# First-layer experts: unscaled tokens against four experts at once, gates applied to the products by VectorE, the eight products summed by GpSimd

## The chip, the cores and the metric

The kernel runs on one core of a Trainium2 chip. The core has a matrix engine (TensorE, "PE" in the profile; its weight loads are "PEld"), a vector engine (VectorE, "DVE"), a scalar engine (ScalarE, "ACT"), GpSimd ("POOL") and SyncE ("SP"), which here only issues DMAs. Every engine works through its own queue in order. The metric is device microseconds of one execution, and the time of a kernel is the median of its runs.

## The reference, cut to what matters

The input is `x`, 32 images of 56 x 56 pixels with 128 channels in float32, which is 100,352 tokens. Two layers follow each other; each is a mixing step and a feed-forward step with residual sums. The change is in the feed-forward step of the first layer, a mixture of eight experts of which each token uses two:

```python
router_probs = softmax(x @ router_w + router_b)          # x: tokens after a layer norm
top_p, top_i = top_k(router_probs, 2)
top_p = top_p / sum(top_p)
expert_out = einsum('bnd,edc->bnec', x, expert_w) + expert_b   # 8 experts, 128 -> 128
gathered   = take_along_axis(expert_out, top_i[..., None], axis=2)
out        = einsum('bnk,bnkc->bnc', top_p, gathered)
t = t + out
```

The kernel computes all eight experts for every token and lets the gates of the six unused ones be zero, so that for a token n the result is the sum over e of gate[n, e] * (x[n] @ expert_w[e]). Around this step lie, in the first layer, a 3 x 3 convolution of signs after a batch norm over the whole input, and in the second layer a triangle product per image and a second set of experts that pick tokens.

## The kernel before, in words

The tokens are cut into 112 units of 896 tokens, and a unit into seven tiles of 128 tokens (`N7 = 7`). Seven units are a pair of images. A first pass over all units computes the statistics of the batch norm; it ends at about 350 us. Then come 16 pairs, which overlap like a pipeline, and at the end the experts of the second layer for all images.

The order of the instructions on each engine is not that of the code. Every stage registers operations with `@op(engine, cost in ns, reads, writes)`, and a planner (class `Order`) simulates the engines with these costs, takes the ready operation of the smallest rank, and writes out the fixed order. The ranks come from the table `TICK`, one number per stage and unit, with 14 ticks from one pair to the next. Buffers come from tagged pools: eight PSUM banks (`ps`), five tiles of 128 x 1024 float32 (`gb`), five unit tiles (`u`), twelve `x` tiles, and so on; an operation whose tile finds no free buffer waits.

For a pair the stages that matter here are:

- `moe_stats` (statistics by `bn_stats`, L484, and a chain of small VectorE instructions, L504 to L546), `moe_turn` (ScalarE normalizes, L558, TensorE transposes, L473, ScalarE copies to `xT`, L579), and `moe_route`, which ends with `gg`, the gates of 14 x 128 tokens for eight experts, tokens on the partitions.
- `moe_gates`, once a unit: TensorE transposes the unit's gates (L793), ScalarE copies them (L800) and issues a DMA to `gate_d` in device memory.
- `moe_experts`, once a tile, so 784 times: a DMA brings the tile's gates back into a `gb` buffer, repeated on all 128 partitions (512 KB each). VectorE multiplies this in place by the transposed tokens (L823). Then eight matmuls, one per expert, add up in PSUM (L828); the scaled tokens are the stationary side and the expert's 128 x 128 weights the moving side. Four tiles share one PSUM bank.
- `moe_add`, twice a unit: VectorE adds the PSUM bank to the residual `x` (L840).

The second layer follows with `tri_stats` and `gate_stats` (the same statistics chains as `moe_stats`), `sign` (VectorE writes the signs into a frame, L607, for the convolution at L629), `tri_out` (L1098, L1107), and `top8`. GpSimd has, in each pair, one memset of `zv` (L1035), one of `a_bd` (L1114) and eight row gathers (L1229), and after the pairs the scatter DMAs of the last experts (L1497). The second layer's experts (`late_experts`) keep their weights in `gb` and `x` buffers and scale rows by `gains` (L1480).

The preparation of the weights makes `expert_w` as one 128 x 1024 tensor, the eight experts side by side; its averages use matmuls with 512 moving columns (L1800).

Of the kernel before, what the change touches and what calls it, by code (L numbers as in the profile page):

```python
# [27 lines left out]
C = 128  # L28
# [9 lines left out]
TICK = {  # L38
    "fetch": (1.14, 2.61, 2.37, -0.16, 7.91, 9.69, 13.32),
    "sign": (0.38, 0.8, 0.81, 5.7, 6.62, 8.09, 11.62),  # L40
    "conv": (2.4, 3.69, 6.8, 7.72, 10.43, 11.89, 12.86),
    "conv_back": (2.88, 4.08, 7.34, 7.86, 10.43, 11.92, 14.91),
    "moe_turn": (4.53, 5.17, 9.52, 8.55, 12.68, 12.47, 15.14),
    "moe_gates": (6.43, 7.52, 9.89, 10.15, 13.98, 12.85, 16.56),
    "moe_experts": (7.18, 7.67, 10.31, 10.83, 14.93, 12.94, 16.8),
    "moe_add0": (10.78, 13.85, 13.48, 12.98, 18.39, 17.9, 18.29),
    "moe_add1": (10.06, 12.78, 13.45, 11.14, 15.45, 13.84, 17.8),
    "tri_turn": (15.73, 17.37, 18.31, 18.26, 19.34, 19.61, 19.71),
    "moe_stats": (4.26, 8.17, 12.25, 14.94),
    "moe_route": (5.48, 9.71, 12.84, 15.88),  # L50
    "tri_stats": (14.82, 13.52, 18.41, 19.02),
    "tri_b": (19.79, 19.99),
    "tri_a": (19.82, 21.57),
    "tri_z": (21.72,),
    "tri_out": (22.38, 23.42, 24.57, 25.03, 26.33, 28.33, 30.18),
    "gate_stats": (23.97, 24.69, 27.63, 30.31),
    "gate_turn": (25.8, 26.15, 26.94, 28.19, 29.43, 32.04, 32.1),
    "gate_logits": (25.91, 27.01, 28.84, 29.87, 31.66, 33.33, 32.83, 33.54),
    "clear": (31.73,),
    "top8": (34.46,),  # L60
    "pool_rows": (37.33,),
    "late_first": (37.82, 37.92, 38.25, 41.79, 42.31, 42.85),
    "late_alone": (51.08, 41.11, 38.24, 41.73, 42.93, 41.08),
    "late_rest": (39.41, 40.01, 40.1, 40.59, 42.76, 44.26, 47.21, 48.79, 50.74, 58.57),
    "last_sums": (49.02,),
    "last_rows": (63.85,),
}
# [216 lines left out]
def kernel(ctx: ExitStack, tc: tile.TileContext, a: dict, out: bass.AP):  # L284
# [101 lines left out]
    z_d = [dram.tile([NV, CH, N7, 2 * H], F32, name=f"z_{p}") for p in range(NP)]  # L386
    gate_d = [dram.tile([N7, E0, 128], F32, name=f"gate_{g}") for g in range(NUT)]

# [14 lines left out]
    with ExitStack() as c2:  # L403
# [19 lines left out]
        for t in lines:  # L423
# [4 lines left out]
            "st": 3, "q": 3, "rT": 1, "lg": 2, "k1": 2, "k2": 2, "mk": 2, "d": 2,  # L428
            "gg": 2, "gT": 2, "rm": 4, "abm": 2, "b": 1, "zq": 1, "zT": 1, "lgT": 1,
            "m8": 2, "i8": 2, "sq": 2, "pg": 2, "near": 2, "pacc": 1, "ptc": 1, "pt": 1,  # L430
# [253 lines left out]
        def moe_route(p, m):  # L684
# [81 lines left out]

            @op("ACT", 210, r=[d], w=[(d, 1)])
            def _():
                nc.scalar.activation(d.ap[:, 1, :], d.ap[:, 0, :], AF.Sigmoid)
                nc.scalar.activation(d.ap[:, 2, :], d.ap[:, 0, :], AF.Sigmoid, scale=-1.0)  # L770
# [11 lines left out]

        def moe_gates(p, u):

            name = f"{p}_{u}"
            m, j = batch_of(u)
            gg = live[p]["gg", m]
            trg = bank(f"trg_{name}")
            gT = new("gT", [N7 * E0, 128], f"gT_{name}")

            @op("PE", 110, r=[gg], w=[trg])
            def _():
                nc.tensor.transpose(  # L793
                    trg.ap[: N7 * E0, :128],
                    gg.ap[:, j * N7 : (j + 1) * N7, :].rearrange("p n e -> p (n e)"), ident,
                )

            @op("ACT", 150, r=[trg], w=[gT])
            def _():
                nc.scalar.copy(gT.ap, trg.ap[: N7 * E0, :128])  # L800

            @op("ACT", 330, r=[gT], w=[("gd", p, u)], land=300)
            def _():
                nc.scalar.dma_start(gate_d[p * NU + u].rearrange("n e q -> (n e) q"), gT.ap)

        def moe_experts(p, u, n):

            name = f"{p}_{u}_{n}"
            xT = live[p]["xT", u]
            if n % 4 == 0:  # L810
                live[p]["acc", u, n // 4] = bank(f"acc_{name}")
            acc = live[p]["acc", u, n // 4]
            gb = new("gb", [C, E0, 128], f"gb_{name}")

            @op("SP", 360, r=[("gd", p, u)], w=[gb], land=1300)
            def _():
                nc.sync.dma_start(
                    gb.ap, gate_d[p * NU + u][n].unsqueeze(0).to_broadcast([C, E0, 128])
                )

            @op("DVE", 1130, r=[(xT, n)], w=[gb])
            def _():
                nc.vector.tensor_tensor(gb.ap, gb.ap, over(xT.ap[:, n, :], E0), ALU.mult)  # L823

            @op("PE", 227 * E0, r=[gb], w=[(acc, n % 4)])
            def _():
                for e in range(E0):
                    nc.tensor.matmul(  # L828
                        acc.ap[:, n % 4 * C : (n % 4 + 1) * C], lhsT=gb.ap[:, e, :],
                        rhs=expert_w[:, e * C : (e + 1) * C], start=(e == 0), stop=(e == E0 - 1),  # L830
                    )

        def moe_add(p, u, q):
            x_, acc = live[p]["x", u], live[p].pop(("acc", u, q))
            k = (4, 3)[q]

            @op("DVE", 60 + 134 * k, r=parts(acc, k), w=parts(x_)[4 * q : 4 * q + k])
            def _():
                dst = x_.ap[:, 4 * q : 4 * q + k, :].rearrange("p n c -> p (n c)")
                nc.vector.tensor_tensor(dst, acc.ap[:, : k * C], dst, ALU.add)  # L840

# [81 lines left out]
        def tri_b(p, h):  # L923

            if h == 0:
                live[p]["b"] = new("b", [128, CH, W], f"b_s_{p}")
            b_s = live[p]["b"]
            u = gated_half(p, "b", h, wb, bb)

            @op("ACT", 540, r=[(u, 0), (u, 4)], w=[(b_s, h)])  # L930
            def _():
                ns = slice(4 * h, min(4 * h + 4, N7))
                nc.scalar.activation(
                    b_s.ap.rearrange("p c (v n) -> p c v n", n=N7)[:, :, :, ns],
                    u.ap[:, :, : (4, 3)[h], :].rearrange("p v n c -> p c v n"), AF.Sigmoid,
                )

        def tri_a(p, h):

            u = gated_half(p, "a", h, wa, ba)  # L940

            @op("ACT", 2 * 500, r=[(u, 0), (u, 4)], w=[("a_bd", h)])
            def _():
# [8 lines left out]
        def tri_z(p):  # L952
# [94 lines left out]
            for j in range(2):  # L1047
                @op("ACT", 750, r=[(zv, rg) for rg in range(4)],
                    w=[("zc", j), ("a_bd", j)])
                def _(j=j):  # L1050
                    nc.scalar.copy(zc[:, j], zv.ap[:, :, j, :].rearrange("c v h -> c h v"))
# [123 lines left out]
        def top8(p):  # L1175
# [32 lines left out]

            @op("ACT", 2700, r=[q, m8], w=all_lg + [(q, 1), (pg, 1)])
            def _():  # L1210
# [725 lines left out]
        for p in range(NP):  # L1936
            for u in range(NU):
# [4 lines left out]
                put(p, "moe_turn", u, moe_turn, p, u)  # L1942
                put(p, "moe_gates", u, moe_gates, p, u)
                for n in range(N7):
# [78 lines left out]
```

## Time and profile before

| what | value |
|---|---|
| median of three runs | 3841.74 us (3836.13 to 3844.88) |
| the profiled execution | 3851.35 us, span 3849.5 us |
| instructions in the span | 77,967 |
| first pass, to about 351 us | PE busy 311.02 us, DVE 299.92 us of 351 us |
| pairs, 351 to 3448 us | PE busy 2940.51 us, DVE 2733.22 us, ACT 1937.06 us, POOL 156.02 us of 3097 us |
| end, from 3448 us | PE busy 244.17 us, DVE 115.92 us, POOL 238.55 us of 401.5 us |
| mean granted TensorE clock | 0.958 of full speed |
| DMA | 811.90 MB in the span; the 784 gate loads are 512 KB each |

Busy time of an engine is the time in which at least one of its instructions was under way; instructions overlap a little at their ends, so that the distance from start to start is below an instruction's own duration. "Idle before" is the time in which the engine had nothing under way, with the event that ended it. The stretch of a pair can be read from the memset at L1114, which comes once a pair: its starts at 838.85 us and 3384.50 us lie 13 pairs apart, 195.8 us each.

### The profile page before, as it was taken

Reading aid. Unit: us, or ns where it says so; the run is one execution under the profiler, and the core shown is the slowest. Engines: PE = TensorE matmul, PEld = TensorE weight load, DVE = VectorE, ACT = ScalarE, POOL = GpSimd, SP = SyncE. Lnnn points to the kernel's source line nnn. Section 1 sums busy time; section 2 is a strip of 40 time slices with the busy share of each in tenths; the row PEclk is TensorE's granted clock in tenths of the full one; section 3 lists DMA queues with packets and bytes.
Section 4 is the critical chain, followed back from the end, with each engine's and each line's share of the span. In section 5 each row is a group of like instructions: output and inputs, shape, how many; then the busy total and the mean of one; then the engine's idle time right before and its main releaser. Section 6 shows DMA issues by size and latency. Waiting matters only on the chain.

```text
span 3849.5 us, 77967 instructions
## 1 busy us (share of the span) xinstructions
PE 3495.7 (91%) x27661; PEld 2836.7 (74%) x27661; DVE 3149.1 (82%) x10452; ACT 2355.4 (61%) x5458; POOL 407.0 (11%) x472
## 2 busy tenths in 40 slices
PE   7999999999999999999999999999999999997653
PEld 6886787777777777778787868686878787865442
DVE  7997879898989898989898989898989898875310
ACT  5997437566666666675757575757575747566210
POOL 1000000100000000000000000101010101003667
PEclk9999999999999999999999999999999999998776
DMA  7997556465656565656565656565656565656774
GB/s 252 349 342 257 199 176 243 174 235 183 230 183 229 176 225 186 224 190 220 191 224 188 219 182 223 188 230 189 230 189 218 201 217 203 203 195 187 211 199 73
DMA packets 325544, 811.90 MB, mean 211 GB/s; under 512 B 86170, under 2 KB 110659, under 8 KB 325155
## 3 DMA queue, kind: packets, MB, share of 16 engines
q1 hardware_dynamic: 262034, 680.39, 51.4%
q10 hardware_dynamic: 41104, 109.20, 7.3%
q0 software_dynamic: 22016, 17.32, 3.1%
q8 instruction: 220, 3.60, 0.4%
q14 instruction: 170, 1.38, 0.1%
HBM read 630.19 MB, written 176.55 MB: 210 GB/s over the span
## 4 chain that ended last, share of the span: by engine, by line
PE 39%; DVE 33%; ACT 11%; DMA 9%; issue 4%; POOL 3%; ACTq 0%; another core or an unknown queue 0%; SPq 0%; DVEq 0%; POOLq 0%
PE acc L828 22%; DVE stln L484 8%; DVE gb L823 7%; DMA gb<-gate 4%; DVE sg L1098 3%; PE ps_cv L629 3%; DMA out<-eo_False,picked 3%; PE gram L1673 3%; POOL out L1497 2%; PE tr L473 2%; DVE x L1107 2%; DVE x L571 2%; ACT ym L558 1%; ACT yt L558 1%; PE ps_z L972 1%
## 5 line engine op out<-in xcount | busy, mean ns | idle before, releaser
L828 PE MATMUL acc<-expert_w,gb 128*128 128x128 f32 x12544 | 1443.9, 276 | 25.2 <-DVE gb L823 13.5
L828 PEld LDWEIGHTS acc<-expert_w,gb 128*128 128x128 f32 x12544 | 1415.1, 192 | 67.3 <-DVE gb L823 33.9
L823 DVE TENSOR_TENSOR gb<-gb,xT 128x1024 f32<-128x1024 f32 x784 | 949.4, 1217 | 64.5 <-DMA gb<-gate 61.5
L484 DVE BATCH_NORM_STATS2 stln<-x 128x6 f32<-128x128 f32 x2352 | 576.4, 281 | 1.9
L558 ACT ACTIVATE ym<-x,rmln 128x128 f32<-128x128 f32 x784 | 322.4, 486 | 244.4 <-DVE rmln L546 243.6
L629 PE MATMUL ps_cv<-frame,w_sign 128*128 128x448 bf16 x2016 | 427.5, 362 | 8.4 <-DVE frame L607 8.4
L558 ACT ACTIVATE yt<-x,rmln 128x128 f32<-128x128 f32 x784 | 324.5, 486 | 123.2 <-DVE rmln L546 120.0
L558 ACT ACTIVATE yl<-x,rmln 128x128 f32<-128x128 f32 x784 | 318.6, 487 | 125.9 <-DVE rmln L543 113.3
L629 PEld LDWEIGHTS <-w_sign 128*128 128x128 bf16 x2016 | 196.4, 99 | 188.5 <-issue 23.8
L1229 POOL DMA_INDIRECT rows<-y,near x128 | 122.2, 955 | 1113.5 <-DVE mk L730 1007.0
L1114 POOL MEMSET a_bd<- 128x2048 f32 x16 | 29.5, 1841 | 1846.3 <-PE ps_zo L1085 1400.7
L840 DVE TENSOR_TENSOR x<-acc,x 128x512 f32<-128x512 f32 x224 | 137.9, 616 | 95.7 <-PE acc L828 95.6
L1497 POOL DMA_INDIRECT out<-eo_False,picked x128 | 197.1, 1540 | 139.0 <-DMA out<-eo_False,picked 74.8
L558 ACT ACTIVATE y<-x,rm 128x128 f32<-128x128 f32 x448 | 194.7, 486 | 20.2 <-DVE rm L543 11.3
L637 ACT ACTIVATE cv<-ps_cv,cv_shift,cv_scale 128x448 f32<-128x448 f32 x224 | 157.9, 725 | 74.8 <-PE ps_cv L629 74.3
L1063 PEld LDWEIGHTS ps_g<-wg,yT 128*128 128x128 f32 x1568 | 187.7, 193 | 21.6 <-issue 15.1
L1063 PE MATMUL ps_g<-wg,yT 128*128 128x128 f32 x1568 | 203.5, 280 | 0.0
L484 DVE BATCH_NORM_STATS2 st<-x 128x6 f32<-128x128 f32 x784 | 179.6, 278 | 24.5 <-DMA x<-in_x 24.2
L1673 PE MATMUL gram<-y 128*128 128x128 f32 x1568 | 196.7, 278 | 0.0
L1673 PEld LDWEIGHTS gram<-y 128*128 128x128 f32 x1568 | 192.3, 198 | 0.0
L579 ACT COPY xT<-trm 128x512 f32<-128x512 f32 x224 | 108.6, 528 | 98.9 <-PE trm L473 79.4
L473 PE MATMUL tr<-ident,y 128*128 128x128 f32 x784 | 139.2, 295 | 29.1 <-ACT y L558 23.1
(244 smaller groups left out, 5295.0 us busy)
## 6 DMA issues: line engine op xcount, KB each, us to landing
gb<-gate SPq DMA_DIRECT2D x784, 512.0 KB
x<-in_x SPq DMA_DIRECT2D x224, 448.0 KB
y<-yT SPq DMA_DIRECT2D x112, 448.0 KB
ys<-y SPq DMA_DIRECT2D x112, 448.0 KB
out<-x ACTq DMA_DIRECT2D x112, 448.0 KB
y<-yl ACTq DMA_DIRECT2D x112, 448.0 KB
w_False<-in_L_ffn_weight SPq DMA_DIRECT2D x128, 256.0 KB
w_True<-in_L_ffn_weight SPq DMA_DIRECT2D x48, 256.0 KB
```

Source lines behind the costliest of these rows:

```text
L473: nc.tensor.transpose(ps.ap[:, n * 128 : (n + 1) * 128], get()[:, n0 + n, :], ident)
L484: nc.vector.bn_stats(st.ap[:, c0 + k, :], src.ap[:, k, :])
L558: nc.scalar.activation(dst.ap[:, k, :], src.ap[:, k, :], AF.Identity, bias=m, scale=r)
L629: nc.tensor.matmul(acc, lhsT=w_sign[:, tap, :], rhs=frames[f][:, 8 * band + kh : 8 * band + kh + 8, kw : kw + W], start=(tap == 0), stop=( ...
L637: nc.scalar.activation(cv.ap[:, :, 64 * h : 64 * h + 64], ps.ap[:, :448].rearrange("c (q n) -> c n q", n=N7), AF.Identity, bias=cv_shift, ...
L823: nc.vector.tensor_tensor(gb.ap, gb.ap, over(xT.ap[:, n, :], E0), ALU.mult)
L828: nc.tensor.matmul(acc.ap[:, n % 4 * C : (n % 4 + 1) * C], lhsT=gb.ap[:, e, :], rhs=expert_w[:, e * C : (e + 1) * C], start=(e == 0), stop ...
L840: nc.vector.tensor_tensor(dst, acc.ap[:, : k * C], dst, ALU.add)
L1063: nc.tensor.matmul(psg.ap[:, n * C : (n + 1) * C], lhsT=yT[:, n0 + n, 16 * u : 16 * u + 16, :].rearrange("c r v -> c (r v)"), rhs=wg, star ...
L1229: nc.gpsimd.indirect_dma_start(out=rows.ap[:, j, :], out_offset=None, in_=y3_d[p], in_offset=bass.IndirectOffsetOnAxis(ap=near.ap[:, k + j ...
L1497: ins = nc.gpsimd.indirect_dma_start(out=tokens_out, out_offset=bass.IndirectOffsetOnAxis(ap=picked[lot][:rows, e : e + 1], axis=0), in_=e ...
L1673: nc.tensor.matmul(gram.ap[:, :C], lhsT=y.ap[:, n, :], rhs=y.ap[:, n, :], start=(g % G16 == 0 and n == 0), stop=(g % G16 == G16 - 1 and n ...
```

## The change

`moe_gates`, the tensor `gate_d` and the gate loads go. In `moe_experts` the unscaled transposed tokens of a tile become the stationary side of two matmuls with 512 moving columns, four experts at once, each into a PSUM bank of its own. VectorE multiplies each bank by the gates, taken from `gg` and repeated along the 128 channels, into a half of a `scaled` tile, which takes the `gb` buffers. GpSimd adds the eight parts with three instructions of 512, 256 and 128 elements a partition into `sum`, a unit tile. `moe_add` adds `sum` to the residual on GpSimd, where VectorE added a PSUM bank before. The pool of `gg` grows from two to three tiles. Five of the planner's costs for ScalarE are raised, and the table `TICK` has new numbers, so the order on all engines is a new one.

```diff
@@ TICK: every row has new numbers; the row "moe_gates" goes @@
@@ buffers @@
-            "gg": 2, "gT": 2, "rm": 4, ...
+            "gg": 3, "rm": 4, ...
@@ moe_route, tri_b, tri_a (and, in the same way, 750 to 1650 in tri_z, 2700 to 4300 in top8): ScalarE's costs for the planner @@
-            @op("ACT", 210, r=[d], w=[(d, 1)])
+            @op("ACT", 430, r=[d], w=[(d, 1)])
-            @op("ACT", 540, r=[(u, 0), (u, 4)], w=[(b_s, h)])
+            @op("ACT", (960, 780)[h], r=[(u, 0), (u, 4)], w=[(b_s, h)])
-            @op("ACT", 2 * 500, r=[(u, 0), (u, 4)], w=[("a_bd", h)])
+            @op("ACT", 2 * 900, r=[(u, 0), (u, 4)], w=[("a_bd", h)])
...
@@ moe_gates goes: transpose, copy, DMA to gate_d @@
@@ moe_experts @@
-            @op("SP", 360, r=[("gd", p, u)], w=[gb], land=1300)
-                nc.sync.dma_start(
-                    gb.ap, gate_d[p * NU + u][n].unsqueeze(0).to_broadcast([C, E0, 128]))
-            @op("DVE", 1130, r=[(xT, n)], w=[gb])
-                nc.vector.tensor_tensor(gb.ap, gb.ap, over(xT.ap[:, n, :], E0), ALU.mult)
-            @op("PE", 227 * E0, r=[gb], w=[(acc, n % 4)])
-                for e in range(E0):
-                    nc.tensor.matmul(
-                        acc.ap[:, n % 4 * C : (n % 4 + 1) * C], lhsT=gb.ap[:, e, :],
-                        rhs=expert_w[:, e * C : (e + 1) * C], start=(e == 0), stop=(e == E0 - 1))
+            if n == 0:
+                live[p]["sum", u] = unit_tile(f"sum_{p}_{u}")
+            total = live[p]["sum", u]
+            scaled = new("gb", [128, E0, C], f"scaled_{name}")
+            half = E0 // 2
+            for h in range(2):
+                acc = bank(f"acc_{name}_{h}")
+                es = slice(half * h, half * h + half)
+                @op("PE", 870, r=[(xT, n)], w=[acc])
+                    nc.tensor.matmul(
+                        acc.ap, lhsT=xT.ap[:, n, :],
+                        rhs=expert_w[:, half * h * C : half * (h + 1) * C], start=True, stop=True)
+                @op("DVE", 640, r=[acc, gg], w=[(scaled, h)])
+                    nc.vector.tensor_tensor(
+                        scaled.ap[:, es, :], acc.ap.rearrange("p (e c) -> p e c", e=half),
+                        along(gg.ap[:, j * N7 + n, es], C), ALU.mult)
+            @op("POOL", 1800, r=[(scaled, 0), (scaled, 1)], w=[(total, n)])
+                t = scaled.ap
+                nc.gpsimd.tensor_tensor(t[:, 0:4], t[:, 0:4], t[:, 4:8], ALU.add)
+                nc.gpsimd.tensor_tensor(t[:, 0:2], t[:, 0:2], t[:, 2:4], ALU.add)
+                nc.gpsimd.tensor_tensor(total.ap[:, n, :], t[:, 0], t[:, 1], ALU.add)
@@ moe_add, k = 4 or 3 tiles @@
-            @op("DVE", 60 + 134 * k, r=parts(acc, k), w=parts(x_)[4 * q : 4 * q + k])
-                dst = x_.ap[:, 4 * q : 4 * q + k, :].rearrange("p n c -> p (n c)")
-                nc.vector.tensor_tensor(dst, acc.ap[:, : k * C], dst, ALU.add)
+            @op("POOL", 80 + 250 * k, r=parts(total)[4 * q : 4 * q + k],
+                w=parts(x_)[4 * q : 4 * q + k])
+                dst = x_.ap[:, 4 * q : 4 * q + k, :]
+                nc.gpsimd.tensor_tensor(dst, total.ap[:, 4 * q : 4 * q + k, :], dst, ALU.add)
```

## The prediction

> **What bounds the kernel now.** I read the page's first part for the engines, then busy time by stretches of one pair, then the groups, then the timeline around single instructions.
>
> ```profile
> PE 3495.7 (91%) x27661; PEld 2836.7 (74%) x27661; DVE 3149.1 (82%) x10452; ACT 2355.4 (61%) x5458; POOL 407.0 (11%) x472
> ```
>
> ```profile
> 1033.68:1228.87 195.19, 186.33 (x1514) 152.48 (x1513) 175.08 (x550) 125.68 (x282) 10.99 (x10) 0.98 0.59 207
> sum 1566.39, PE 1488.97 PEld 1214.96 DVE 1394.97 ACT 1004.83 POOL 87.81; mean PE 186.12 PEld 151.87 DVE 174.37 ACT 125.60 POOL 10.98
> ```
>
> The columns are the stretch, its length, and the busy time of PE, PEld, DVE, ACT and POOL, then granted clock and DMA. The sum is over eight pairs, 195.8 us each. TensorE is busy 186.1 us of a pair and idle 9.7; VectorE is busy 174.4 and idle 21.4. So TensorE sets the pace and VectorE stands 12 us behind it: whatever the change does to either counts, and 12 us more on VectorE turns the bound over. GpSimd has nearly nothing to do. The first 351 us hold none of the changed work.
>
> **TensorE's part.** The timeline and the groups give the two kinds of matmul:
>
> ```profile
> 1266.12 9.20 PE L828 MATMUL acc<-expert_w,gb 128*128 128x128 f32 x80 [0.19 <-DVE gb L823]
> ```
>
> ```profile
> L1800 PE MATMUL ps_mean_e<-e_raw,mean_w x4: 592/594/595, 24.2 to 29.7; 128*128 128x512 f32 x4
> ```
>
> A float32 matmul is two instructions. In a row, one with 128 columns costs 9.20/80 = 0.115 us, so a tile costs 16 x 0.115 = 1.84 us (the `gb` instructions alone have TensorE busy 90.3 us for 49 tiles, the same). With 512 columns an instruction lasts 594 ns against 275 ns (the minimum of L828), 0.83 ns a column; in a row I take 115 + 384 x 0.83 = 434 ns, and a tile needs four, 1.74 us. The change saves 0.107 us a tile, 5.2 us for the 49 tiles of a pair, and with seven gate transposes (0.11 to 0.13 us each) 6.1 us: 180 us a pair remain. The weight loads become fewer and were beside the matmuls anyway.
>
> **VectorE's part, by its own work.**
>
> ```profile
> 1212.91 0.67 DVE L840 TENSOR_TENSOR x<-acc,x 128x512 f32<-128x512 f32 x1
> 1213.52 1.21 DVE L823 TENSOR_TENSOR gb<-gb,xT 128x1024 f32<-128x1024 f32 x1
> ```
>
> An instruction that reads 512 elements from PSUM and 512 from SBUF holds VectorE 0.61 us from start to start; L1480, with a repeated scalar as in the new product, has nearly the same duration (690 ns against 682). Removed in a pair: 59.3 us of L823 and 8.6 us of L840, 67.9 us. Added: 98 x 0.61 = 59.8 us. VectorE would come to 174.4 - 67.9 + 59.8 = 166.3 us.
>
> **GpSimd's part.** No row has a two-input GpSimd instruction. The nearest are the memsets: 1841 ns for 2048 elements, 1610 for 1792, so 0.90 ns an element for a single stream. An add has two streams in and one out, so its bounds are 0.9 and 2.7 ns an element. I take 1.8 (two reads one after the other) and 0.1 us for each instruction (the 1 x 1 memset at 3469.61 us took 0.09): 1.02, 0.56 and 0.33 us, 1.91 us a tile, and 1.81 us for the two residual adds of a unit. A pair has 49 x 1.91 + 7 x 1.81 = 106 us, 151 us at the upper bound and 61 at the lower; with 11 us of memsets and gathers it fits into 195 us.
>
> The Trainium skill ("GPSIMD Engine Reference", Elementwise — side-by-side cycle accounting) gives 4497 ns for a float32 add of 2048 elements, 2.2 ns each. By it a tile would be an estimated 2.0 to 2.3 us, 5 to 20% above mine; no run here shows it yet.
>
> **What the two engines do to each other.** This decides. The trace has both engines waiting for one another:
>
> ```profile
> 1228.87 1.81 POOL L1114 MEMSET a_bd<- 128x2048 f32 x1 [109.93 <-PE ps_zo L1085]
> 1312.37 1.61 POOL L1035 MEMSET zv<- 128x1792 f32 x1
> 3540.36 2.32 POOL L1497 DMA_INDIRECT out<-eo_False,picked  x1 [1.23 <-DMA out<-eo_False,picked]
> ```
>
> ```profile
> 1219.30 1.27 DVE L607 TENSOR_SCALAR frame<-ys,bn_scale,bn_limit 128x896 bf16<-128x896 f32 x1
> 1229.48 0.26 DVE L734 TENSOR_TENSOR k<-k,rev 128x112 f32<-128x112 f32 x1
> 1312.86 1.95 DVE L607 TENSOR_SCALAR frame<-ys,bn_scale,bn_limit 128x896 bf16<-128x896 f32 x1
> 3540.13 1.08 DVE L1107 TENSOR_TENSOR x<-sg,x 128x896 f32<-128x896 f32 x1
> ```
>
> Start, duration, engine. A frame write takes 1.27 us alone and 1.95 when it meets the memset of 1312.37; it ends 0.83 us after that. In most pairs the same two meet, with about 2.0 us. The scatter at 3540.36 lasts 2.32 us against a median of 1.55, for it met L1107, a VectorE add of two SBUF tensors that ended at 3541.21. And the two-input L734 of 0.26 us was not held by the memset of 1228.87. So there is a wait between some VectorE instructions and some GpSimd ones, as long as the instruction in front, and a memset, which reads nothing, spares VectorE's two-input instructions. No row has a GpSimd instruction that streams from SBUF beside VectorE. The change puts 106 us of those into each pair.
>
> The Trainium skill ("SBUF — State Buffer", Who interferes with whom) says that a VectorE instruction with two SBUF inputs contends with a GpSimd instruction that reads SBUF, and waits for the whole of it. The three rows above agree with it as far as they go; it speaks against this change.
>
> The price. By the counts of the lines, a pair has 223 VectorE instructions with two SBUF inputs that stay (13 in each of 12 statistics chains, 11 in each of 4 routings, 9 in `tri_z`, 7 at L1107, 7 at L1249) and 34 tensor_scalars like L607: 257. The bounds of a wait are 0, and nothing below it since no row shows an instruction shortened, and the whole add in front, 1.02 us; all 257 at that would be 262 us a pair, out of reach while GpSimd is free for half of the time. I work out the middle: one that comes at random finds GpSimd in an add with a chance of 106/222 = 0.48, and then waits half the length-weighted duration, (1.02² + 0.56² + 0.33²) / (2 x 1.91) = 0.38 us. That is 0.18 us each and 257 x 0.18 = 47 us a pair. VectorE would need 166.3 + 47 = 213 us; I add the 9.7 us of idle that the bounding engine has now, and get 223 us, 27.1 us more than now. A dependent chain that meets the start of the next add each time would wait nearer 0.64 x 0.5 = 0.3 us; its instructions are most of the 257, so the range goes above rather than below.
>
> **What else moves.** The 49 gate loads and seven DMA issues and copies of a pair go; the waits for gate loads are 61.5 us in the whole run, and most of that turns into waits for PSUM products on an engine with idle time, so I count it at nothing; the cover is VectorE's 21 us of idle, and if that is gone it is at most 61.5/16 = 4 us a pair. Behind GpSimd's gathers (8 x 1.25 us) and memsets the adds now queue, and behind the adds the gathers; `scaled` has five buffers, 6 us of VectorE's products, so up to 4 us a pair may show. `sum` holds one of five unit buffers for a unit's expert time. The costs and ranks cost nothing themselves; the end after 3448 us has the same work in another order, to which I give 0, and 20 us either way.
>
> **The sum.** The pairs fill 3097 us, 15.8 times 195.8. 15.8 x 27.1 = 428 us on the profiled execution's 3851.35 is 4279; the median lies 9.6 us below that execution, so **4270 us**. What a measurement here can tell from no change is about 0.2%, 8 us.
>
> **Rivals.**
> - *No wait between the adds and VectorE.* Then TensorE bounds: 186.1 - 6.1 + 9.7 = 189.7 us a pair, 96 us less in all, 3745 us; faster. VectorE at 166 us is far off. For it: no row has an add beside VectorE, and L734 was not held. Against it: the frame writes and the scatters. The point of decision is VectorE's 166.3 + 9.7 + waits = 195.8: waits under 20 us a pair, 0.08 us for each of the 257, leave it no slower.
> - *GpSimd becomes the bound.* 151 us by 2.7 ns, and 0.3 us between instructions as between the gathers (161 adds, 48 us) make 199 us, with the 14 us of gathers, their gaps and memsets 213; without VectorE's waits that is 17 us a pair more, about 4110 us; with 0.1 us less of each gap, 3860. For it: three dependent adds a tile. Against it: the middle price.
> - *The waits are full ones.* At 0.3 us for 257, 77 us: 253 us a pair, 57 us more, 4740 us.
>
> **How the numbers follow.** The forecast with waits of 0.12 to 0.27 us, 4015 to 4630 us: 0.70. GpSimd as the bound, or weaker waits of 0.08 to 0.12 us, 3850 to 4110: 0.10. Full waits above 4640: 0.06. No waits, faster: 0.13; a balance within 0.2%: 0.01. The range is 3840 to 4640 us; the faster case and the dearest waits are left out, 0.2 together. Slower by over 0.2% has 0.86.
>
> **What would show it.** Right: in the stretch of a pair TensorE's busy time falls to about 180 us while the stretch grows beyond 215; L504 and L505, 0.17 us on average now, have durations of 0.3 us and more, with maxima near the length of an add, and `bn_stats` (one input) stays at 0.28; POOL stands near 106 to 130 us a pair. Wrong: those lines unchanged, and a pair of 190 us. The step that I trust least is the share of instructions that really meet an add: if the chains fall where GpSimd is idle, the sum halves.

## The result, and the profile after

The changed kernel takes 4469.07 us (median of four runs, 4466.32 to 4473.66), the kernel before 3843.31 us on the same chip: a ratio of 1.163 (95% interval 1.160 to 1.166). The profiled execution took 4473.66 us, 622 us more than the one of before.

The first part of the page after, and two rows of its second part (tenths of busy time in 40 slices, and the granted clock):

```profile
PE 3693.0 (83%) x18141; PEld 2088.1 (47%) x18141; DVE 3686.7 (82%) x11012; ACT 2338.5 (52%) x5348; POOL 2669.0 (60%) x3048
POOL 0005665666656565666675857666666656675657
PEclk9999899998989898989999999989899989997786
```

No engine is over 83% of the span. GpSimd has gone from 407 to 2669 us. One pair by stretches, in the same columns as for before, with three stretches of 10 us out of it and, from the same view, ten pairs in one:

```profile
1227.04:1462.58 235.54, 201.11 (x917) 106.67 (x917) 210.54 (x585) 124.35 (x273) 152.52 (x173) 0.91 0.19 61
1227.04:3577.26 2350.22, 2004.98 (x9170) 1061.63 (x9170) 2096.87 (x5841) 1244.30 (x2730) 1527.92 (x1712) 0.91 0.19 61
1267.00:1277.00 10.00, 10.00 (x70) 5.21 (x68) 7.49 (x32) 9.98 (x23) 0.00 (x0) 1.00 0.30 101
1347.00:1357.00 10.00, 9.49 (x39) 4.92 (x36) 9.45 (x22) 0.11 (x1) 9.45 (x11) 0.83 0.12 47
1357.00:1367.00 10.00, 8.95 (x58) 5.30 (x57) 10.00 (x29) 2.06 (x4) 9.53 (x11) 1.00 0.09 34
```

A pair takes 235.0 us instead of 195.8. That is all of the loss: 15.8 pair-lengths times 39.2 us are 619 of the 622 us. The last two stretches show what the averages hide: GpSimd, 65% busy over a pair, stands at 95% and has no room while the experts of a unit run, and has nothing at all to do in others (1267 to 1277). VectorE is busy 209.7 us of a pair and idle 25.3; TensorE is no longer the bound.

The groups that the change made, and `bn_stats` beside them (count, then busy us and mean ns of one, then the idle time before them and what ended it):

```profile
L797 PE MATMUL acc<-expert_w,xT 128*128 128x512 f32 x3136 | 1520.9, 625 | 76.1 <-DVE scaled L804 58.8
L812 POOL TENSOR_TENSOR scaled<-scaled 128x512 f32<-128x512 f32 x784 | 1013.3, 1292 | 736.9 <-DVE scaled L804 612.6
L804 DVE TENSOR_TENSOR scaled<-acc,gg 128x512 f32<-128x512 f32 x1568 | 1014.0, 681 | 145.0 <-POOL sum L814 111.0
L813 POOL TENSOR_TENSOR scaled<-scaled 128x256 f32<-128x256 f32 x784 | 615.5, 785 | 61.5
L482 DVE BATCH_NORM_STATS2 stln<-x 128x6 f32<-128x128 f32 x2352 | 565.0, 279 | 86.4 <-POOL x L824 85.9
L814 POOL TENSOR_TENSOR sum<-scaled 128x128 f32<-128x128 f32 x784 | 402.3, 513 | 73.4 <-POOL scaled L813 11.1
```

The three adds of a tile last 1.29, 0.79 and 0.51 us on average. VectorE now waits for GpSimd in two places that before did not exist: over the whole run 111.0 us for a free `scaled` buffer and 85.9 us for the residual add before the next statistics; in the ten pairs it is 9.7 of the 25.3 us of idle time a pair. The single lines that the prediction named (shortest, median and longest duration in ns):

```profile
L503 DVE TENSOR_TENSOR q_ln<-q_ln,rmln x384: 145/166/1252, 367.4 to 4174.0; 128x14 f32<-128x14 f32 x144, 128x7 f32<-128x7 f32 x48
L503 DVE TENSOR_TENSOR zq<-zq x32: 216/766/1244, 607.0 to 4111.2; 128x56 f32<-128x56 f32 x32
L482 DVE BATCH_NORM_STATS2 stln<-x x2352: 263/279/349, 359.7 to 4166.1; 128x6 f32<-128x128 f32 x196
L812 POOL TENSOR_TENSOR scaled<-scaled x784: 1253/1268/2131, 389.2 to 4059.6; 128x512 f32<-128x512 f32 x196
```

L503 (L505 of before) has kept its median of 0.166 us on `q_ln`, but its longest is 1.25 us, the length of an add (0.19 before); on the tile `zq`, in a chain that falls among the adds nearly every time, the median itself has gone from 0.206 to 0.766 us. `bn_stats`, with one input, stays at 0.279. Of the kernel before, the same line:

```profile
L505 DVE TENSOR_TENSOR q_ln<-q_ln,rmln x384: 141/166/192, 368.4 to 3547.4; 128x14 f32<-128x14 f32 x144, 128x7 f32<-128x7 f32 x48
L505 DVE TENSOR_TENSOR zq<-zq x32: 194/206/216, 562.7 to 3490.5; 128x56 f32<-128x56 f32 x32
```

And the timeline shows waits in both directions:

```profile
1240.61 1.27 POOL L812 TENSOR_TENSOR scaled<-scaled 128x512 f32<-128x512 f32 x1
1240.87 1.04 DVE L541 SCALAR_TENSOR_TENSOR rmln<-q_ln,rmln 128x14 f32<-128x14 f32 x1
1245.22 1.25 DVE L605 TENSOR_SCALAR frame<-ys,bn_scale,bn_limit 128x896 bf16<-128x896 f32 x1
1245.34 1.45 POOL L814 TENSOR_TENSOR sum<-scaled 128x128 f32<-128x128 f32 x1
```

A VectorE instruction of 14 elements with two inputs, 0.17 us in the median, takes 1.04 us and ends 0.03 us after the add in front of it. An add of 128 elements, 0.46 us alone, takes 1.45 us and ends 0.32 us after the frame write.

### The profile page after: what moved, and what is told of

It reads as the page before. It is cut to its first block, busy times and chain, and to the rows that moved or that the text cites. A ratio compares the mean times of both kernels' runs of the same rounds, so it can differ in the third digit from the quotient of the medians.

```text
span 4471.9 us, 60929 instructions
## 1 busy us (share of the span) xinstructions
PE 3693.0 (83%) x18141; PEld 2088.1 (47%) x18141; DVE 3686.7 (82%) x11012; ACT 2338.5 (52%) x5348; POOL 2669.0 (60%) x3048
## 5 line engine op out<-in xcount | busy, mean ns | idle before, releaser
L797 PE MATMUL acc<-expert_w,xT 128*128 128x512 f32 x3136 | 1520.9, 625 | 76.1 <-DVE scaled L804 58.8
L812 POOL TENSOR_TENSOR scaled<-scaled 128x512 f32<-128x512 f32 x784 | 1013.3, 1292 | 736.9 <-DVE scaled L804 612.6
L804 DVE TENSOR_TENSOR scaled<-acc,gg 128x512 f32<-128x512 f32 x1568 | 1014.0, 681 | 145.0 <-POOL sum L814 111.0
L797 PEld LDWEIGHTS acc<-expert_w,xT 128*128 128x128 f32 x3136 | 590.7, 201 | 711.8 <-issue 426.7
L813 POOL TENSOR_TENSOR scaled<-scaled 128x256 f32<-128x256 f32 x784 | 615.5, 785 | 61.5
L482 DVE BATCH_NORM_STATS2 stln<-x 128x6 f32<-128x128 f32 x2352 | 565.0, 279 | 86.4 <-POOL x L824 85.9
L814 POOL TENSOR_TENSOR sum<-scaled 128x128 f32<-128x128 f32 x784 | 402.3, 513 | 73.4 <-POOL scaled L813 11.1
L824 POOL TENSOR_TENSOR x<-sum,x 128x512 f32<-128x512 f32 (+1 forms) x224 | 262.4, 1182 | 8.1
L1057 ACT ACTIVATE sg<-ps_g 128x512 f32<-128x512 f32 x224 | 118.0, 541 | 249.8 <-PE ps_g L1047 221.4
L471 PE MATMUL trm<-ident,ym 128*128 128x128 f32 x784 | 160.6, 317 | 100.4 <-ACT ym L556 99.9
L471 PE MATMUL trt<-ident,yt 128*128 128x128 f32 x784 | 132.2, 295 | 130.2 <-ACT yt L556 111.1
```

What stands on the lines that cost most here:

```text
L471: nc.tensor.transpose(ps.ap[:, n * 128 : (n + 1) * 128], get()[:, n0 + n, :], ident)
L482: nc.vector.bn_stats(st.ap[:, c0 + k, :], src.ap[:, k, :])
L797: nc.tensor.matmul(acc.ap, lhsT=xT.ap[:, n, :], rhs=expert_w[:, half * h * C : half * (h + 1) * C], start=True, stop=True,)
L804: nc.vector.tensor_tensor(scaled.ap[:, es, :], acc.ap.rearrange("p (e c) -> p e c", e=half), along(gg.ap[:, j * N7 + n, es], C), ALU.mult,)
L812: nc.gpsimd.tensor_tensor(t[:, 0:4], t[:, 0:4], t[:, 4:8], ALU.add)
L813: nc.gpsimd.tensor_tensor(t[:, 0:2], t[:, 0:2], t[:, 2:4], ALU.add)
```

## The experiments

The theory before the experiments was that of the prediction: VectorE's two-input instructions wait behind adds that read SBUF. Its rival was that GpSimd cannot serve the tiles as fast as they come, whatever it does to VectorE. Pairs are measured between the starts of the `a_bd` memset, over ten pairs; idle is the pair less VectorE's busy time. "A tile" is the distance from one tile's first GpSimd instruction to the next tile's, in rows where nothing else comes between; "reads" means that its instructions read SBUF. The residual adds, two a unit, are GpSimd instructions that read SBUF in the changed kernel and in all that are made from it, except the one with its sum on VectorE. The kernel before was run again beside each group of experiments, at 3845 to 3855 us; the ratios are to those runs.

| kernel | a tile on GpSimd, us | pair, us | VectorE busy / idle, us | time, us |
|---|---|---|---|---|
| before | none | 195.8 | 174.3 / 21.4 | 3843.31 |
| changed | 2.57, reads | 235.0 | 209.7 / 25.3 | 4469.07 |
| one memset of 128 for the adds | 0.15 | 192.0 | 176.3 / 15.7 | 3788.98 |
| memsets 1024, 128 | 1.04 | 193.2 | 177.0 / 16.2 | 3818.52 |
| memsets 1024, 512, 128, 128 | 1.88 | 197.2 | 176.4 / 20.8 | 3874.95 |
| memsets 1024, 1024, 256, 128 | 2.42 | 217.4 | 177.5 / 40.0 | 4206.07 |
| memsets 1024, 1024, 512, 128 | 2.63 | 225.4 | 179.0 / 46.3 | 4329.04 |
| adds of 256 and 128 only | 1.22, reads | 199.3 | 183.1 / 16.2 | 3900.20 |
| first add on VectorE | 1.22, reads | 243.2 | 216.6 / 26.6 | 4572.45 |
| sum on VectorE | none | 228.3 | 208.9 / 19.4 | 4366.28 |
| GpSimd's measured costs for the planner | 2.57, reads | 241.0 | 214.3 / 26.7 | 4568.11 |
| ranks of before | 2.57, reads | 269.6 | 192.2 / 77.4 | 5012.18 |
| before, with idle adds | 2.68, reads | 265.4 | 234.6 / 30.8 | 4978.52 |
| before, with idle memsets | 3.16 | 230.0 | 181.8 / 48.2 | 4388.01 |

**Adds that read nothing.** The three adds became memsets of somewhat more than their duration.

```diff
-                nc.gpsimd.tensor_tensor(t[:, 0:4], t[:, 0:4], t[:, 4:8], ALU.add)
-                nc.gpsimd.tensor_tensor(t[:, 0:2], t[:, 0:2], t[:, 2:4], ALU.add)
-                nc.gpsimd.tensor_tensor(total.ap[:, n, :], t[:, 0], t[:, 1], ALU.add)
+                nc.gpsimd.memset(t, 0.0)
+                nc.gpsimd.memset(t, 0.0)
+                nc.gpsimd.memset(t[:, 0:4], 0.0)
+                nc.gpsimd.memset(total.ap[:, n, :], 0.0)
```

> The changed kernel, but the three GpSimd adds of a tile are four memsets of 1024, 1024, 512 and 128 elements (about 2.4 us, as long as the adds); the eight products are not summed. Theory 'waits for reads': VectorE instructions with two SBUF inputs wait for GpSimd instructions that read SBUF, and a memset reads nothing; then the 30 to 35 us a pair of their waits go, VectorE's busy time falls from 210 to about 178 us a pair, and a pair takes 197 to 208 us, 3880 to 4050 us in all. Rival 'load and order': GpSimd's 2.5 us a tile, the five product buffers and the order of the queues set the pace, whatever GpSimd does in that time; then a pair stays at 230 to 235 us, 4400 to 4470 us.

Measured: 4329.04 us, ratio 1.126 [1.122, 1.129], between the two ranges. The lengthening of VectorE's instructions over their means of before, summed over all that exist in both kernels, fell from 579 us to 146 us, as the theory of waits has it, but the time fell by only 140. So the waits alone are not the cause. The stretch of ten pairs, and the largest of VectorE's waits over the whole run (us in all, times, longest):

```profile
1198.15:3451.67 2253.52, 1994.53 (x9170) 1062.11 (x9170) 1790.31 (x5841) 1246.75 (x2730) 1539.40 (x2201) 0.91 0.20 64
DVE stln L482 <- POOL x L825: 361.8, 92, 11.3
```

VectorE has only 179 us of work in a pair of 225 and spends much of the rest waiting for the residual add, which stands in GpSimd's queue behind the tiles.

**No sum at all.** One memset of 128 elements takes the place of the three adds.

> The changed kernel without the sum: GpSimd only clears the 128-element result of a tile (0.12 us); the eight products are not summed. Both theories: TensorE bounds again, 188 to 198 us a pair, 3730 to 3880 us in all. It prices everything that the adds do, and shows whether the wide matmuls alone would have been faster than the kernel before (the forecast's faster rival, 3745 us). If it stays above 4000 us, the cost is neither in the waits nor in GpSimd's load but in the two PSUM banks a tile or the new order.

Measured: 3788.98 us, ratio 0.985 [0.982, 0.988]. That is the change without GpSimd's adds, and the time lies in the range expected: by the ratio 58 us faster than before, TensorE at 92% of the span, 185.8 us of a pair. A lengthening of 94 us is left in it; the residual adds are the GpSimd instructions that still read.

```profile
PE 3466.8 (92%) x18141; PEld 2018.6 (53%) x18141; DVE 3180.2 (84%) x11012; ACT 2330.0 (62%) x5348; POOL 783.3 (21%) x1480
```

**Shorter memsets, and a part of the adds that reads.** Two memsets (1024 and 128 elements) that read nothing, and in another kernel the last two adds alone, at nearly the same pace.

```diff
@@ short memsets @@
+                nc.gpsimd.memset(t, 0.0)
+                nc.gpsimd.memset(total.ap[:, n, :], 0.0)
@@ half of the adds @@
-                nc.gpsimd.tensor_tensor(t[:, 0:4], t[:, 0:4], t[:, 4:8], ALU.add)
-                nc.gpsimd.tensor_tensor(t[:, 0:2], t[:, 0:2], t[:, 2:4], ALU.add)
+                nc.gpsimd.tensor_tensor(t[:, 0:2], t[:, 0:2], t[:, 4:6], ALU.add)
```

> The changed kernel, GpSimd's three adds of a tile replaced by two memsets of 1024 and 128 elements, about 1.25 us a tile where the adds take 2.56 and TensorE's matmuls 1.74; the eight products are not summed. Theory 'pace' (the memsets as long as the adds gave 4329 us and none 3789, because in a burst of experts GpSimd is slower than TensorE, and TensorE stands until buffers come free): below TensorE's 1.74 us the pace is TensorE's again, 3790 to 3900 us. Rival 'share' (each us of GpSimd work costs the same, through queues and ports, 3789 + 540 x 1.25/2.6): 4020 to 4080 us.

> The changed kernel with two of the three adds, of 256 and 128 elements, about 1.28 us a tile; four of the eight products are left out. As much GpSimd time as the run with two short memsets, but it reads. Theory 'pace': GpSimd keeps up with TensorE, and only VectorE's waits for reads remain, at half the share and for shorter adds (0.73 and 0.46 us): about 8 to 12 us a pair on a VectorE with 12 us to spare, so 3820 to 3980 us, 0 to 100 us above the short memsets. If waits for reads alone decide: half of 622 us, 4100 to 4180 us.

Measured: 3818.52 us (0.990 [0.987, 0.993]) and 3900.20 us (1.011 [1.008, 1.015]), each in the range of the pace theory and outside its rival's. With less than half of the changed kernel's GpSimd time for a tile the loss is nearly gone. Reading is worth at most 82 us here, 6 us of VectorE's busy time a pair; the tiles that read also take 0.2 us longer.

**Where the pace begins to cost.** Two more lengths of memsets: 1024, 512, 128, 128, and 1024, 1024, 256, 128, whose 2.42 us a tile is close to the 2.57 us of the adds.

> The three adds of a tile are replaced by memsets of 1024, 512, 128 and 128 elements (the sum is left out), which by the memsets measured so far take about 1.95 us a tile; they read nothing. Pace theory (GpSimd serves a tile's work within the part of a pair that holds the experts, about 0.63 x 195.8 = 123 us or 2.5 us for each of 49 tiles with nothing else in its queue, less the gathers and residual adds, so about 2.1 us a tile): below that point nothing is lost, and the time is 3820 to 3920 us. Rival, a loss in proportion to GpSimd's work: on the line through 1.25 us a tile (3818.5) and 2.75 us a tile (4329) it is about 4050 us (4000 to 4100).

> The three adds of a tile are replaced by memsets of 1024, 1024, 256 and 128 elements (the sum is left out), about 2.55 us a tile as the adds of the changed kernel take (2.56), but they read nothing. If GpSimd's pace is only one of two limits that lie close together, it alone gives 209 to 219 us a pair (between a line through 1.95 and 2.75 us a tile, 197 and 225 us, and a slope of 49 tiles over 0.63 of a pair below 225): 4060 to 4230 us, and VectorE's waits make the rest of the changed kernel's 235 us. Rival, the pace alone is the whole: 232 to 238 us a pair, 4420 to 4520 us.

Measured: 3874.95 us (1.005 [1.004, 1.007]) and 4206.07 us (1.091 [1.089, 1.094]). The first is far below the proportional rival's 4050: there is a pace up to which GpSimd's work is nearly free. The second lies inside the 4060 to 4230 us of the theory of two limits. The stretches of ten pairs of the two:

```profile
1085.90:3058.17 1972.27, 1891.48 (x9170) 1017.17 (x9170) 1763.62 (x5841) 1243.66 (x2730) 1165.98 (x2201) 0.97 0.23 73
```

```profile
1166.27:3340.75 2174.48, 1960.74 (x9170) 1049.28 (x9170) 1774.66 (x5841) 1245.47 (x2730) 1428.37 (x2202) 0.93 0.21 66
```

VectorE's work is the same in both, 176.4 and 177.5 us a pair; only GpSimd's has grown, from 116.6 to 142.8, and the pair with it from 197.2 to 217.4. From 1.04 to 1.88 us a tile the pair grows by 5 us for each us more, from 1.88 to 2.42 by 37, from 2.42 to 2.63 by 38: the point is near 1.9. Carried to 2.57 the line gives 223 us. So GpSimd's pace alone, with nothing read for a tile, is worth about 27 of the 39 us. The theory's reason for the point (the share of a pair in which experts run) is not shown: a limit that holds all 49 tiles would have a slope of 49 or more, not 38. The profiles show where the time goes: of VectorE's idle time, waits for GpSimd are nothing at 1.04 us a tile, 6.1 us a pair at 1.88, 22.1 at 2.42 and 27.2 at 2.63.

**The same adds in the kernel before.** Idle adds on `xT`, seven tiles' worth for each unit, their result unused, and the same with a copy of one element and five memsets of 512 elements in place of each tile's adds; one `x` buffer fewer makes room.

```diff
+        def moe_junk(p, u):
+            xT = live[p]["xT", u]
+            for n in range(N7):
+                @op("POOL", 2560, r=parts(xT), w=["junk"])
+                def _():
+                    t = xT.ap
+                    nc.gpsimd.tensor_tensor(junk, t[:, 0:4], t[:, 3:7], ALU.add)
+                    nc.gpsimd.tensor_tensor(junk[:, 0:2], t[:, 0:2], t[:, 3:5], ALU.add)
+                    nc.gpsimd.tensor_tensor(junk[:, 0], t[:, 0], t[:, 1], ALU.add)
```

> The kernel before with idle work for GpSimd: for each tile three adds of 512, 256 and 128 elements that read the transposed tokens and write a scratch tile which nobody reads; one x buffer fewer (11), to make room. Theory 'waits for reads': 223 + 49 two-input instructions and 34 tensor_scalars a pair wait 0.15 us or more each, VectorE rises from 174 to 215 us or more and bounds: 225 to 245 us a pair, 4300 to 4650 us. Rival 'load and order': nothing waits for these adds, so at most 2% above the kernel before, 3840 to 3920 us.

> As the run with idle adds, but GpSimd's work for a tile is a copy of one element and five memsets of 512 elements, about 2.4 us as well; the same 11 x buffers and nearly the same order. Theory 'waits for reads': only the 34 tensor_scalars a pair meet the memsets, VectorE rises by 5 to 15 us a pair, which TensorE's pace mostly hides: 3850 to 3980 us. Rival 'load and order': the same time as the run with idle adds, within 1%.

Measured: 4978.52 us (1.294 [1.291, 1.298]) and 4388.01 us (1.141 [1.137, 1.144]). Both missed: the first lies above either range, the second fits neither theory. Their first parts:

```profile
PE 3962.4 (80%) x27661; PEld 3088.9 (62%) x27661; DVE 4100.0 (82%) x10452; ACT 2368.7 (48%) x5456; POOL 2821.0 (57%) x2824
```

```profile
PE 3777.9 (86%) x27661; PEld 2953.1 (67%) x27661; DVE 3247.0 (74%) x10452; ACT 2358.5 (54%) x5456; POOL 2872.7 (65%) x5176
```

GpSimd is as busy in the one as in the other, and VectorE has 853 us more with the adds that read; its instructions are lengthened by 891 us against 73. The 590 us between the two are the price of reading at such a load, if the pace weighs no less in the second (its tiles take 3.16 us, those of the first 2.68). But the run with the memsets is itself 543 us slower than before. That the gathers queue behind the memsets and that these hold `xT` may be the reason; it is not shown. The missing `x` buffer has a part too, which was not measured alone: VectorE waits 4.2 us a pair for loads of `x` there, and in the kernel before not at all. As a test of waits alone the pair was a poor one.

**The planner told what GpSimd takes.** The costs of the adds go from 1800 to 2560 ns, those of the residual add from 80 + 250 k to 220 + 280 k.

> The changed kernel, whole, with the planner's two costs of GpSimd set to what the profile shows: 2560 ns a tile instead of 1800, and 220 + 280 k ns for the residual adds. The planner writes out another order; no instruction is changed. Theory 'pace': the order written for 1.8 us puts the experts in bursts that GpSimd can't follow; with the true cost other work is put between them, and the time falls to 4200 to 4400 us; VectorE's waits for reads, about 37 us a pair, remain and keep it above 4100. Rival 'the waits set it': no gain beyond 1%, 4430 to 4500 us.

Measured: 4568.11 us, ratio 1.185 [1.181, 1.188], 99 us slower than the changed kernel; both theories' numbers are missed. VectorE's instructions are lengthened by 686 instead of 579 us: the other order did not thin out the adds in front of VectorE. Its idle time a pair is 26.7 instead of 25.3 us, but of another kind. The waits for GpSimd, 9.7 us a pair in the changed kernel, are nearly gone (0.2), as the pace theory has it; waits for TensorE (12.5 us instead of 7.3) and ScalarE (8.9 instead of 4.4) have taken their place, and why is not shown. The rows over ten pairs, two of the changed kernel and the first of this kernel's two (us in all, times, longest):

```profile
DVE scaled L804 <- POOL sum L814: 62.5, 50, 2.1
DVE stln L482 <- POOL x L824: 33.6, 24, 1.8
DVE scaled L804 <- POOL scaled L812: 0.9, 4, 0.2
```

**The ranks of before.** The changed kernel with the old table `TICK`.

> The changed kernel with the rank table of the kernel before (without its row of the gates). If the new ranks are what crowds GpSimd's adds into two thirds of a pair, the time falls by 100 us or more, to below 4370. If the pace is set by what a tile costs GpSimd and by VectorE's waits, whatever the ranks, it stays within 100 us of 4469, since the old ranks put the experts into about the same part of a pair (7.18 to 16.8 of 14 ticks).

Measured: 5012.18 us, ratio 1.300 [1.298, 1.303]. Neither case: it is 543 us slower than with the new ranks. The ten pairs, and VectorE's largest wait in them:

```profile
1341.61:4037.55 2695.94, 2122.57 (x9171) 1093.47 (x9171) 1922.17 (x5841) 1258.33 (x2730) 1475.73 (x1711) 0.87 0.16 54
DVE stln L483 <- POOL x L825: 357.2, 70, 11.3
```

VectorE's instructions wait less behind GpSimd's (VectorE is busy 192.2 us a pair, its lengthening 329 us), and idle time took the place of that: 77.4 us a pair, 36 of them for the residual add. So the order decides much more than was thought, and the new ranks are part of what keeps the loss at 16%.

**The first add on VectorE**, the whole computation:

```diff
-                nc.gpsimd.tensor_tensor(t[:, 0:4], t[:, 0:4], t[:, 4:8], ALU.add)
+            @op("DVE", 600, r=[(scaled, 0), (scaled, 1)], w=[(scaled, 0)])
+            def _():
+                t = scaled.ap
+                nc.vector.tensor_tensor(t[:, 0:4], t[:, 0:4], t[:, 4:8], ALU.add)
@@ the two adds that stay become an operation of their own: POOL, 1280 @@
```

> The whole computation; the first of the three adds (512 elements) goes to VectorE, two adds (256 and 128) stay with GpSimd, 1.28 us a tile. If GpSimd's pace per tile was the larger part of the loss, that part goes, and VectorE takes 49 two-input adds of 512 elements, 0.6 us each, 29 us a pair: 166.3 + 3.6 + 29.4 = 199 us of own work, with waits of 10 to 20 us and idle of 10 us a pair of 219 to 229 us: 4200 to 4360 us, below the changed kernel. Rival, waits of two-input instructions as the larger part: there are 49 more of them, each may meet an add, and VectorE would come to 199 + 40 + 10 = 249 us a pair: above 4600 us.

Measured: 4572.45 us, ratio 1.187 [1.185, 1.189]; the first theory's range missed by 212 us, the rival's by 28. Ten pairs, the added instruction in them, and VectorE's two largest waits:

```profile
1192.52:3624.31 2431.79, 2089.40 (x9171) 1100.13 (x9170) 2166.12 (x6331) 1251.40 (x2730) 1012.03 (x1221) 0.90 0.18 59
L812 DVE TENSOR_TENSOR scaled<-scaled 128x512 f32<-128x512 f32 x490 | 382.3, 800 | 0.2
DVE m L1175 <- ACT lgT L1157: 93.2, 10, 10.6
DVE x L569 <- PE trc L471: 58.2, 21, 5.2
```

The 49 adds take 38.2 us a pair, 0.68 us each alone and 0.80 on average, where 29 were counted. VectorE is busy 216.6 us, within the 209 to 219 that were foreseen, though with more work of its own and fewer waits. The idle time is the step of this expectation that failed: 26.6 us against 10. Waits for GpSimd are 0.5 us of it; the largest are for ScalarE and for transposes (9.3 and 5.8 us a pair).

**The sum on VectorE**, without GpSimd, the whole computation: eight fused multiply-adds a tile straight from PSUM onto `x`, each with one gate.

```diff
+                for e in range(half):
+                    @op("DVE", 260, r=[acc, gg], w=[(live[p]["x", u], n)])
+                    def _(h=h, acc=acc, e=e):
+                        x_ = live[p]["x", u].ap[:, n, :]
+                        k = half * h + e
+                        nc.vector.scalar_tensor_tensor(
+                            x_, acc.ap[:, e * C : (e + 1) * C],
+                            gg.ap[:, j * N7 + n, k : k + 1], x_, ALU.mult, ALU.add,
+                        )
@@ the scaled products, the three adds, the sum tile and moe_add go @@
```

> A third way, whole: the wide matmuls stay, and VectorE multiplies each expert's 128 columns in PSUM by the gate and adds them to the residual in one instruction, eight a tile, in the planner's order one by one; GpSimd does nothing in it. At 0.26 us each from start to start (as the weighted row sums before) VectorE has 49 x 8 x 0.26 = 102 us a pair in place of 68: 208 us, and with 10 to 20 us idle 218 to 228 us a pair, 4180 to 4350 us: slower than before, and not by GpSimd. If the eight dependent instructions wait for one another (0.38 us each), 149 us, 4700 to 5000 us.

Measured: 4366.28 us, ratio 1.132 [1.129, 1.135], 103 us faster than the changed kernel and 16 us above the first range. With GpSimd at its 111 us in ten pairs, VectorE's busy time is as long as in the changed kernel (208.9 us) and the idle time is 19.4:

```profile
1180.97:3464.18 2283.21, 2017.60 (x9170) 1054.84 (x9170) 2089.43 (x8781) 1256.18 (x2730) 110.94 (x101) 0.92 0.20 63
```

## Why the prediction was right, and where its sum was off

The forecast was 4270 us, slower for the reason that VectorE's instructions would wait behind GpSimd's adds and turn the bound over. The direction holds and the waits are there, but 199 us are missing, and the waits are not the whole mechanism: GpSimd's pace, which the prediction had as a rival, works beside them. Of the signs that it named, the longer pair (235 us, above 215), the maxima of L504 and L505 (L502 and L503 now) near the length of an add and the unchanged `bn_stats` came. TensorE's fall to about 180 us a pair and GpSimd's 106 to 130 us did not (200.5 and 152.8). By its steps:

**TensorE's work: the price right, the saving not, and off the path.** In a row a 512-column instruction takes 0.43 us from start to start, as was said. But the 6.1 us a pair are not seen in TensorE's busy time: without the sum, where TensorE is the bound, it is 185.8 us against 186.0 over the same ten pairs of before, not 180. The instructions of L797 have TensorE busy 91.2 us a pair there, those of L828 had it 90.4. The pair is 3.8 us shorter nearly all because TensorE is less idle (6.2 us instead of 9.8). In the changed kernel TensorE is busy 200.5 us a pair and not 180, at a granted clock of 0.91 instead of 0.98 and with waits of its own. The 96 us of rival one are an upper end: 3745 us were worked out, 3789 measured.

**VectorE's own work: 3.6 us short.** The scaled product takes 1014.0/16 = 63.4 us a pair instead of 59.8, so 169.9 instead of 166.3. In a row two products are 0.60 us apart, as was taken; an instruction lasts 0.68 us, and not all of them stand in a row.

**Waits: the size came out, in part by luck.** 209.7 - 169.9 = 39.8 us a pair, against 47; over the 257 instructions 0.155 us each against 0.18. But the 0.18 is a chance of 0.48 times a wait of 0.38 us, and neither is what the trace has. Of the 223 two-input instructions of a pair 65 are longer than their median of before by more than 0.1 us: a chance of 0.29, with 0.53 us on average for each that meets an add. The adds are longer than was taken and fill 142 us of the pair, not 106; with the measured durations the random count would give a chance of 0.60 times 0.48 us times 257 = 74 us, about the price of the rival with full waits. So GpSimd's price, which was too low, and the random count, which is too high, cancelled each other. The instructions do not come at random: medians stay, some chains meet no add and others meet one nearly every time, as `zq` shows. The Trainium skill ("SBUF — State Buffer", Who interferes with whom) is borne out in both directions: the two-input instruction at 1240.87 us ends with the add, `bn_stats` with its single input does not wait, and memsets, which read nothing, took the lengthening from 579 to 146 us, where 94 are left without any sum.

**Idle time: the term that was mis-sized.** VectorE's 9.7 us, taken over from TensorE, measured 25.3. Together: 3.6 - 7.2 + 15.6 = 12 us above the forecast of 223, the 235 us of a pair; times 15.8, 190 of the 199 us. Two things are in it. An engine that becomes the bound does not inherit the idle time of the one before: the kernel with its sum on VectorE, bound by VectorE with GpSimd nearly free, has 19.4 us. And GpSimd's pace adds to it: 9.7 of the 25.3 us are VectorE's waits for `scaled` buffers and residual adds. They can't simply be taken off, though: with GpSimd's measured costs for the planner they are gone, and the idle time is 26.7 us.

**GpSimd's price: too low.** 1.91 us a tile were taken; the three dependent adds take 2.57 us from start to start (1.27, 0.73 and 0.46 us undisturbed, 2.1 ns an element and 0.19 us for each instruction, and 0.06 to 0.09 us between them). A pair has 152.8 us of GpSimd against 117. The Trainium skill ("GPSIMD Engine Reference", Elementwise — side-by-side cycle accounting) has 4497 ns for one add of 2048 elements. The line through the three adds of this case gives 2.1 x 2.048 + 0.19 = 4.5 us there, so the two agree. The estimate of 2.0 to 2.3 us a tile stays below the 2.46 us that the three take together because it went by the figure for each element of one long add; three short ones pay the 0.19 us three times. This weighs more than its term in the sum: in the memset runs 1.91 us lie at the point from which the pace begins to cost, 2.57 us well above it. The second rival, GpSimd as the bound, was held to be an alternative to the waits, at 213 us a pair. The runs show both at once, and nearly equal: pace alone 223 us (memsets, carried to 2.57 us a tile), waits alone 209.7 + 19.4 = 229 us (an estimate with the idle time of the kernel with its sum on VectorE), both 235. Alone they are 27 and 33 us above the 195.8 of before, together 39: they hide each other in part, and how the 39 us divide is not shown more closely than that.

**What else moves.** The first `a_bd` memset comes at 757.77 us instead of 644.06: the first pair's experts run at the new pace already. After the last one 301 us remain instead of 306, so the end costs nothing.

## What to carry to other kernels

Before work goes to an engine with 90% of its time free, look at how that work comes: an engine that is free on average can be full while one stage runs, and here work that reads nothing was nearly free up to 1.9 us a tile, with GpSimd busy 59% of a pair. Count its price from a row with the same number of inputs and of dependent instructions, and count separately what its reads do to the other engine (here 0.155 us on average for each of 257 VectorE instructions). And when the bound moves to another engine, take that engine's idle time as its own question; here it was written down as 10 us twice and measured as 25 and 27.

## What the runs showed of the hardware that was not expected

- GpSimd is held by VectorE in turn, for which the prediction's sum had no term: the 128-element add at 1245.34 us took 1.45 us behind a frame write. The three adds of a tile last 2.59 us together on average and 2.46 undisturbed, 7 us a pair. In the kernel with the first add on VectorE its 256-element add has a mean of 921 ns instead of 785.
- The granted clock is lower in kernels whose TensorE is idle for more of a pair: 0.97 without the sum (3% idle), 0.91 in the changed kernel (15%), 0.87 with the ranks of before (21%). The order is not strict: with GpSimd's measured costs for the planner it is 0.89 at 13%. In single stretches it is lower still, with TensorE nearly all of the time busy:

```profile
1287.00:1297.00 10.00, 8.75 (x36) 4.28 (x35) 7.84 (x28) 9.92 (x13) 7.70 (x9) 1.00 0.17 47
1297.00:1307.00 10.00, 9.40 (x43) 8.84 (x44) 7.50 (x10) 4.18 (x10) 8.69 (x10) 0.55 0.03 8
```

What sets it there was not tried, nor how much of the 39 us a pair it is.
